# The experts' input turned by DMA for the gate's logits, and a rotary table with each value once

## The chip, the cores and the metric

The kernel runs on one core of a Trainium2 chip. The core has five engines with their own instruction queues: TensorE (PE, matmuls and transposes, with its weight loads listed as PEld), VectorE (DVE), ScalarE (ACT), GpSimd (POOL) and SyncE (SP), which here only issues DMAs. Instructions of one queue start in the order of the program; between queues semaphores order the work. The metric is the time of one execution on the device in microseconds (us); lower is better.

## The reference

One transformer block with adaptive layer norm, for 2 sequences of 2048 tokens with 256 features, all in float32:

```python
mod = (silu(c) @ wmod).reshape(2, 6, 1, -1)
sa, ca, ga, sb, cb, gb = ...                  # ga, gb: kept at least 0.25 away from 0
h = layernorm(x) * (1 + ca) + sa
x = x + ga * attention(h)                     # 2 query heads, 1 key/value head of 128, causal, rotary
h = layernorm(x) * (1 + cb) + sb
x = x + gb * experts(h)

def apply_rope(x):                            # pairs of neighbours are rotated
    out = stack([x0 * cos - x1 * sin, x1 * cos + x0 * sin])

def experts(x):                               # 8 experts, 256 -> 1024 -> 256 with gelu
    gate = softmax(x @ Wg + bg)
    thr = sigmoid(x @ Wt + bt) * 0.125
    w = (gate - thr) where it is >= 0, else 0
    out = sum over e of (w / sum(w))[e] * expert_e(x)
```

Which experts a token goes to follows from the logits `x @ Wg`, so only tokens with a weight above 0 are worked on by an expert.

## The kernel before

**First part: attention and gate.** The 4096 tokens are 32 tiles of 128 (16 for each of 2 sequences, `b` and `i`). `tile_steps(b, i, r, group, g)` adds the steps of one tile to a plan; `r` is the tile's place in the order, 0 to 31. In order: load `x` (SP), moments (`sta`, `mva` on DVE, the reciprocal root `rstda` on POOL), normalise (`xn`, line 459, DVE or POOL), two transposes on PE (`pt`, 468), copies to `hT` with scale and shift (476, 478), the projection to query, key and value (`pq`, 489), the rotation (`rot`: `t` at 505 and 513 on DVE, the addition at 522 on DVE or POOL), three transposes (`pr`, 529), scores (`psc`, 545), softmax (DVE `s`, `nmx`; ACT exponential), transposes of the weights (`ptr`, 618), their product with the values (`pav`, 628), the output projection (`po`, 662), the residual (`x`, 669) and the store of `x` to `out` (678).

Then comes what the change touches. Again moments (`stf`, `mvf`, `rstdf`), and `hx` (685, 688, DVE): the normalised, modulated row, which is the experts' input. It is used twice:

- `halves` (695, POOL) writes `hp`, in which the lower and the upper 16 bits of each float32 stand apart, 256 of the one and then 256 of the other; SP stores it to `feats` in DRAM (702). From there the second part gathers rows by token and has a DMA turn them (a DMA transposes 16-bit elements), and DVE joins the two halves to float32 again.
- `turn_h` (710, PE) transposes `hx` in two blocks of 128x128 into PSUM (`ph`), `hT2_out` (714, ACT) copies that to `hT2`, `logits` (719, PE) multiplies by the gate's weights (`pl`), and `logits_out` (727, DVE) adds the bias to `lg`.

For each group of tiles (four, later two and one) `gate_steps` turns `lg` into weights, counts the tokens of each expert and scatters entries to the experts' lists in DRAM (826, POOL).

**The order.** `Plan.run()` writes the order of all queues ahead of time. Each step has an engine (or several to choose from), a cost in us, buffers that it takes and gives back by name (`room` holds how many there are), steps that it comes after, a rank and, for a DMA, a lag (`late`) until its data is there. Simulated time goes forward, and an idle engine takes the ready step of lowest rank; a step with two engines goes to the first that is idle. These costs are numbers in the code: if one of them changes, the order on every queue may change. The run on the chip keeps the order of each queue and waits for semaphores. Work of lowest priority fills in: the first two items of expert 0 (`pha`, line 975; `pya`, 992) are computed while the last tiles of attention wait.

**Second part: the experts.** `experts()` loops over items of 256 tokens; PE alternates `h` (1202) and `y` (1193), POOL gathers and scatters rows, SP issues a DMA transpose for each item, DVE joins the halves. It begins when the list of expert 0 is complete, some 24 us after the logits of the last tile.

Of the kernel before, what the change touches and what calls it, by code (L numbers as in the profile page):

```python
# [12 lines left out]
F32 = mybir.dt.float32  # L13
BF16 = mybir.dt.bfloat16
I32 = mybir.dt.int32
U16 = mybir.dt.uint16
ET = mybir.EngineType
AF = mybir.ActivationFunctionType
ALU = mybir.AluOpType
AX = mybir.AxisListType  # L20

P = 128
B, T, D = 2, 2048, 256
HS, NH = 128, 2
E, FF = 8, 1024
KD = D // P
NF = FF // P
NT = T // P
NTOK = B * T
# [14 lines left out]
class Plan:  # L44
# [10 lines left out]
    def add(self, eng, cost, do, after=(), take=(), give=(), rank=0.0, late=0.0):  # L55

        if isinstance(eng, str):
            eng, cost, do = [eng], [cost], lambda _, do=do: do()  # L60
        self.steps.append((eng, cost, do, tuple(after), tuple(take), tuple(give), rank, late))
        return len(self.steps) - 1
# [140 lines left out]
def attention(  # L203
# [5 lines left out]
    nc = tc.nc  # L209
    PSUM = bass.MemoryType.PSUM  # L210
    ctx = ExitStack()
    room = {"ps": 6, "pav": 2, "x": 9, "s": 16, "pT": 3, "hx": 4, "hp": 3, "qT": 3, "big": 3, "xn": 3,
            "hT": 2, "hT2": 2, "aT": 2, "g_sb": 1, "sign": 1, "size": 1, "ga": 1}
    const = ctx.enter_context(tc.tile_pool(name="const_a", bufs=1))
    pool = ctx.enter_context(tc.tile_pool(name="work", bufs=3))
    small = ctx.enter_context(tc.tile_pool(name="small", bufs=8))
# [3 lines left out]
    def ps_tile(name):  # L220
        return psum.tile([P, 512], F32, tag="ps", name=name)

    def work(shape, tag, u, dtype=F32):
        return pool.tile(shape, dtype, tag=tag, name=f"{tag}{u}", bufs=room.get(tag, 3))
# [5 lines left out]
    of = {"DVE": nc.vector, "POOL": nc.gpsimd}  # L230
    first = -100.0
# [18 lines left out]
    modT = const.tile([P, 2 * KD, B], F32, name="modT")  # L250
    mod_bc = const.tile([P, B, 2 * D], F32, name="mod_bc")
    woG = const.tile([P, B, NH, D], F32, name="woG")
    rope_sb = const.tile([P, NT, 2, HS], F32, name="rope_sb")
    c_sb = const.tile([P, KD, B], F32, name="c_sb")
    sc = const.tile([P, KD, B], F32, name="sc")

# [25 lines left out]
    def load(dst, src, kb, rank=first, **how):  # L282
        return plan.add(
            "SP", max(0.5, kb / 360.0), lambda: nc.sync.dma_start(dst, src), late=2.0, rank=rank,
            **how
        )
# [5 lines left out]
    l_qkv = load(wqkv_sb, wqkvT.rearrange("(k p) f -> p k f", p=P), 512, rank=first - 1)  # L292
    l_rope = [
        load(rope_sb[:, ds(4 * q, 4)], rope.rearrange("(q n p) (z f) -> p q n z f", p=P, n=4, z=2)[:, q],
             512, rank=first if q == 0 else q * 8 - 7.5)
        for q in range(NT // 4)
    ]

# [51 lines left out]
    for b in range(B):  # L350
# [43 lines left out]
        r = 1.6 + 3 * b  # L394
# [6 lines left out]
    for e in range(RES):  # L401
# [3 lines left out]
                rank=8.0 + 4 * e,  # L405
# [12 lines left out]
    def moments(u, st, after, add):  # L418


        def stats():
            six = little([P, 6], "st", u)
            nc.vector.bn_stats(six, st["x"])
            st["mv"] = little([P, 2], "mv", u)
            nc.vector.bn_aggr(st["mv"], six)  # L425

        def rstd():
            st["rstd"] = little([P, 1], "rstd", u)
            nc.gpsimd.tensor_scalar(st["rstd"], st["mv"][:, 1:2], EPS, None, ALU.add)  # L429
            nc.gpsimd.tensor_tensor(st["rstd"], st["rstd"], neg_half, ALU.pow)  # L430

        n = add("DVE", 0.62, stats, after)
        return add("POOL", 0.85, rstd, [n])

    def tile_steps(b, i, r, group, g):

        u = f"_{b}_{i}"
        st = {}
# [4 lines left out]
        def add(eng, cost, do, after=(), **how):  # L443
            return plan.add(eng, cost, do, after=after, rank=r, **how)
# [10 lines left out]
        n_n = moments("a" + u, st, [n_x], add)  # L455
# [4 lines left out]
                st["xn"], st["x"], st["mv"][:, 0:1], st["rstd"], ALU.subtract, ALU.mult  # L460
            )

        n_n = add(["DVE", "POOL"], [0.42, 0.65], xn, [n_n], take=["xn"])

        def turn():
            st["pt"] = ps_tile(f"pt{u}")
# [13 lines left out]
        n_t = add("PE", 0.32, turn, [n_n], take=["ps"], give=["xn"])  # L480
# [18 lines left out]
        def rot(z):  # L499
            dst = st["t", z] = work([P, 3, HS], f"t{z}", u)  # L500
            table = rope_sb[:, i, z, :]
            src = st["pq"][:, : 3 * HS]
            if z == 0:
                src = src.rearrange("p (h f) -> p h f", h=3)
                nc.vector.tensor_tensor(
                    dst, src, table.unsqueeze(1).to_broadcast([P, 3, HS]), ALU.mult
                )
            else:
                src = src.rearrange("p (h j two) -> p h j two", h=3, two=2)
                d4 = dst.rearrange("p h (j two) -> p h j two", two=2)  # L510
                t4 = table.rearrange("p (j two) -> p j two", two=2)
                for y in range(2):
                    nc.vector.tensor_tensor(
                        d4[:, :, :, y], src[:, :, :, 1 - y],
                        t4[:, :, y].unsqueeze(1).to_broadcast([P, 3, HS // 2]), ALU.mult,
                    )

        n_r0 = add("DVE", 0.6, lambda: rot(0), [n_q, l_rope[i // 4]], take=["big"])
        n_r1 = add("DVE", 0.75, lambda: rot(1), [n_q, n_v, n_r0], give=["ps"])
# [16 lines left out]
        n_t = add("PE", 0.48, turn_rot, [n_r], take=["ps"], give=["big"])  # L536
# [43 lines left out]
        for h in range(NH):  # L580
            kept = []
            for c in range(nch):
# [4 lines left out]
                    give=["qT"] if (h, c) == (NH - 1, nch - 1) else [],  # L587
# [47 lines left out]
        for c0 in range(0, i + 1, 2):  # L635
# [3 lines left out]
            n_t = add(  # L639
                "PE", 0.12 * 2 * m, lambda c0=c0, m=m: turn_p(c0, m), [n_e[0, c], n_e[1, c]],  # L640
                take=["ps"] + (["pav"] if c0 == 0 else []), give=["s", "s"] if done else [],
            )
            n_o = add(
                "ACT", 0.2 + 0.26 * m, lambda c0=c0, m=m: pT_out(c0, m), [n_t], take=["pT"],
                give=["ps"],
# [35 lines left out]
        n_n = moments("f" + u, st, [n_x2], add)  # L681
# [10 lines left out]
        n_h = add("DVE", 0.97, hx, [n_n, m_mod[b], n_st], take=["hx"], give=["x"])  # L692
        def halves():
# [2 lines left out]
                st["hp"], st["hx"].bitcast(U16).rearrange("p (d two) -> p two d", two=2)  # L696
            )

        n_f = add("POOL", 1.2, halves, [n_h], take=["hp"])
        add(  # L700
            "SP", 0.8,
            lambda: nc.sync.dma_start(
                feats[ts(b * NT + i, P), :], st["hp"].rearrange("p two d -> p (two d)")
            ), [n_f], late=2.0, give=["hp"],
        )

        def turn_h():
            st["ph"] = ps_tile(f"ph{u}")
            for k in range(KD):
                nc.tensor.transpose(st["ph"][:, ts(k, P)], st["hx"][:, ts(k, P)], ident)  # L710

        def hT2_out():
            st["hT2"] = work([P, KD, P], "hT2", u)
# [12 lines left out]
                group["lg"] = little([P, 4, E + 1], "lg", u)  # L726
            nc.vector.tensor_tensor(group["lg"][:, g, :], st["pl"][:, : E + 1], bgt_sb, ALU.add)

        n_t = add("PE", 0.32, turn_h, [n_h], take=["ps"])
        n_t = add("ACT", 0.38, hT2_out, [n_t, n_f], take=["hT2"], give=["ps", "hx"])  # L730
        n_t = add("PE", 0.5, logits, [n_t, l_wg], take=["ps"], give=["hT2"])
        return add("DVE", 0.17, logits_out, [n_t, l_bg], give=["ps"])

# [119 lines left out]
    begun, q = [0] * B, 0  # L853
# [93 lines left out]
    for k in range(AHEAD):  # L947
        st = {}

        def columns(k=k, st=st):  # L950
# [4 lines left out]
            lambda c, k=k: kept.front[:, k * CI + c, 2:3].bitcast(I32), f"_{k}",  # L955
# [53 lines left out]
        for f0 in range(0, NF, 2):  # L1009
# [4 lines left out]
                take=["ps"], give=["s"] if f0 == NF - 2 else [],  # L1014
# [3 lines left out]
                take=["s"], give=["ps"],  # L1018
            ))
        n = None  # L1020
        for c in range(CI):
            for f0 in (0, NF // 2):
# [3 lines left out]
                    take=["ps"] if (c, f0) == (0, 0) else [],  # L1026
                    give=["s"] * (NF // 2) if (c, f0) == (CI - 1, NF // 2) else [],
# [424 lines left out]

def _rope_table():


    at = np.arange(0, HS, 2, dtype=np.float32)
    theta = np.float32(10000.0) ** (np.float32(-2.0) * at / np.float32(HS))
    angles = np.arange(T, dtype=np.float32)[:, None] * theta[None, :]
    cos, sin = np.cos(angles), np.sin(angles)
    both = np.stack([cos, cos], axis=-1), np.stack([-sin, sin], axis=-1)  # L1460
    return np.concatenate([a.reshape(T, HS) for a in both], axis=1).astype(np.float32)


# [35 lines left out]
```

## Time and profile before

| What | Value |
|---|---|
| Median of 5 runs | 1645.23 us (1644.44 to 1646.55) |
| The profiled execution: time, span from its first to its last instruction | 1644.22 us, 1642.4 us |
| Mean granted clock of TensorE | 0.996 |
| First part: from 0 to the first `h` matmul | 486.5 us |
| PE busy from 123 to 410 us | 284.9 of 287 us |
| `ph`: 64 transposes on PE | 12.8 us busy, 281 ns each |
| `hT2`: 32 copies on ACT | 11.8 us busy, 370 ns each |
| `hp`: 32 copies on POOL | 19.6 us busy, 612 ns each |
| Second part: `h` and `y` matmuls | 657.9 and 654.2 us busy |

How to read it: busy time of an engine is the time in which an instruction of it is listed as running. Matmuls overlap, so the listed time of one is longer than the time for which it keeps PE from the next; the distance between two starts tells more. Idle time of an engine is given with what ended it (after `<-`). "PE 9 tenths" means that at least 90% of a slice is busy.

### The profile page before, as it was taken

The numbers are of one execution on the slowest core, as the hardware profiler recorded it, in microseconds if no ns is written. First come the engines' busy times: TensorE is split into PE (matmuls) and PEld (weight loads), VectorE is DVE, ScalarE is ACT, GpSimd is POOL, SyncE is SP. The second block draws the span as 40 slices with busy tenths as digits, with TensorE's granted clock in tenths as the row PEclk, the third lists the DMA queues.
The fourth block names the chain that finished last, engine by engine and source line by source line (L and its number), as shares of the span: only waits on it lengthen the run. The fifth ranks groups of instructions, "written<-read, shape, count | busy, mean of one in ns | idle before, by whom it ended". The sixth has DMA issues, their size and how long they took to land.

```text
span 1642.4 us, 26732 instructions
## 1 busy us (share of the span) xinstructions
PE 1613.0 (98%) x7666; PEld 1346.4 (82%) x7666; DVE 656.9 (40%) x2144; ACT 584.5 (36%) x1417; POOL 908.7 (55%) x1032
## 2 busy tenths in 40 slices
PE   8999999999989999999999999999999999999997
PEld 5666776777778888888888888888888888888886
DVE  6987666666532233223223222222222232222322
ACT  3555665655532232222223222222222222222322
POOL 5575333231127767757766775675777477644443
PEclk9999999999999999999999999999999999999999
DMA  5411000010023353335335333533534343333333
GB/s 184 151 40 37 23 30 23 19 42 14 14 68 67 62 116 65 58 65 111 57 68 113 59 58 61 108 60 59 110 58 66 58 59 60 65 58 55 66 56 48
DMA packets 165950, 106.35 MB, mean 65 GB/s; under 512 B 111041, under 2 KB 157249, under 8 KB 165761
## 3 DMA queue, kind: packets, MB, share of 16 engines
q0 software_dynamic: 41968, 46.83, 17.9%
q1 hardware_dynamic: 116048, 46.22, 12.3%
q10 hardware_dynamic: 7872, 12.58, 2.4%
q8 instruction: 26, 0.43, 0.1%
q14 instruction: 36, 0.29, 0.1%
HBM read 50.39 MB, written 31.86 MB: 50 GB/s over the span
## 4 chain that ended last, share of the span: by engine, by line
PE 69%; issue 0%; DMA 0%; DVE 0%; POOLq 0%; POOL 0%; DVEq 0%
PE h L1202 35%; PE y L1193 34%; DMA out<-yo,who 0%; POOLq L1143 0%; DVE yo L1295 0%; DVE xT L924 0%; POOL out L1352 0%; DVE xT L1256 0%; DVE yb L1280 0%; DVEq L1495 0%; POOLq L1445 0%; POOLq L1352 0%; DVE who L1286 0%; POOLq L1312 0%; POOLq L1447 0%
## 5 line engine op out<-in xcount | busy, mean ns | idle before, releaser
L1202 PE MATMUL h<-xT,w 128*128 128x256 f32 (+1 forms) x2752 | 657.9, 372 | 4.8 <-DVEq L1306 4.7
L1193 PE MATMUL y<-w,g 128*128 128x256 f32 x2640 | 654.2, 379 | 0.0
L1228 ACT ACTIVATE g<-h,b_sb 128x256 f32<-128x256 f32 (+1 forms) x688 | 320.4, 466 | 835.3 <-PE h L1202 833.1
L1202 PEld LDWEIGHTS h<-xT,w 128*128 128x128 f32 x2752 | 513.0, 191 | 74.3 <-DVEq L1306 5.1
L1193 PEld LDWEIGHTS y<-w,g 128*128 128x128 f32 x2640 | 498.7, 190 | 66.2
L1352 POOL DMA_INDIRECT out<-yo,who x172 | 282.6, 1643 | 207.1 <-DVE yo L1295 154.7
L1256 DVE COPY xT<-xp 128x512 uint16<-128x512 uint16 x172 | 68.6, 440 | 609.7 <-PE h L1202 605.0
L1342 POOL DMA_INDIRECT list<-new,to x216 | 220.2, 1019 | 93.6 <-POOL new L1337 44.2
L1318 POOL DMA_INDIRECT xr<-feats,at x172 | 173.9, 1011 | 100.5 <-POOL at L1363 70.5
L545 PE MATMUL psc<-kT,qT 128*128 128x512 f32 (+3 forms) x320 | 143.4, 534 | 0.0
L628 PE MATMUL pav<-pT,v 128*128 128x256 f32 x544 | 142.6, 384 | 0.0
L628 PEld LDWEIGHTS pav<-pT,v 128*128 128x128 f32 x544 | 96.0, 190 | 29.6 <-issue 19.9
L556 DVE TENSOR_SCALAR_CACHE_REDUCE s<-psc 128x512 f32<-128x512 f32 (+3 forms) x160 | 95.2, 604 | 62.3 <-PE psc L545 48.0
L1280 DVE TENSOR_TENSOR yb<-y,b_bc 128x256 f32<-128x256 f32 x165 | 62.6, 419 | 136.1 <-PE y L1193 136.1
L572 ACT ACTIVATE s<-s,nmx 128x512 f32<-128x512 f32 (+3 forms) x160 | 103.9, 651 | 36.9 <-DVE nmx L563 36.7
L622 ACT COPY pT<-ptr 128x512 f32<-128x512 f32 (+1 forms) x144 | 76.5, 564 | 51.7 <-PE pav L628 33.2
L826 POOL DMA_INDIRECT list<-entry,place x40 | 42.5, 1063 | 72.7 <-DVE place L823 43.4
L1271 DVE SCALAR_TENSOR_TENSOR gate<-gb_bc,mcur,part 128x256 f32<-128x256 f32 x172 | 75.8, 481 | 3.0
L618 PEld LDWEIGHTS ptr<-ident,s 128*128 128x128 f32 x544 | 63.4, 142 | 14.3 <-ACT s L572 4.6
L618 PE MATMUL ptr<-ident,s 128*128 128x128 f32 x544 | 72.4, 274 | 2.1 <-ACT s L572 1.9
L1363 POOL COPY at<-sheet 128x2 int32 x85 | 63.7, 749 | 14.7 <-DMA xp<-xr 14.7
L429 POOL TENSOR_SCALAR rstdf<-mvf 128x1 f32<-128x1 f32 x32 | 8.5, 264 | 113.6 <-DVE mvf L425 86.4
(165 smaller groups left out, 1101.4 us busy)
## 6 DMA issues: line engine op xcount, KB each, us to landing
w<-in_w ACTq DMA_DIRECT2D x12, 1024.0 KB, 7.9
x<-in_x SPq DMA_DIRECT2D x32, 128.0 KB, 2.1
out<-x SPq DMA_DIRECT2D x32, 128.0 KB, 1.7
feats<-hp SPq DMA_DIRECT2D x32, 128.0 KB, 1.7
w<-in_w SPq DMA_DIRECT2D x4, 1024.0 KB, 8.5
list<-new,to POOLq DMA_INDIRECT x216
xr<-feats,at POOLq DMA_INDIRECT x172
out<-yo,who POOLq DMA_INDIRECT x172, 3.9
```

The costliest lines, as they stand in the source:

```text
L545: nc.tensor.matmul(ps[:, :w], st["qT"][:, h, :], kT[:, ds(c * SC, w)], start=True, stop=not last)
L556: nc.vector.tensor_scalar(s[:, :w], st["sc", h, c][:, :w], 1.0, None, ALU.mult, ALU.max, accum_out=st["mx", h][:, c : c + 1],)
L572: nc.scalar.activation(s[:, :w], s[:, :w], AF.Exp, bias=st["nmx", h], accum_out=st["den"][:, h, c : c + 1],)
L618: nc.tensor.transpose(ptr[:, j, h, :], s[:, ds((c0 + j) * P % SC, P)], ident)
L622: nc.scalar.copy(pT[:, :m], st["ptr", c0][:, :m])
L628: nc.tensor.matmul(st["pav"][:, : NH * P], v[:, c0 + j, :], st["pT", c0][:, j].rearrange("p h t -> p (h t)"), start=(c0 + j == 0), stop=(c ...
L1193: last = pe.matmul(ys[c], gs[f % 4][:, ts(c, P)], weights[e][1][:, f, :], start=(f == 0), stop=(f == NF - 1),)
L1202: last = pe.matmul(hs[f % 4][:, :w], weights[e][0][:, k, ts(f, P)], xT[:, k, :w], start=(k == 0), stop=(k == KD - 1),)
L1228: act.activation(gs[f % 4][:, :w], hs[f % 4][:, :w], AF.Gelu_apprx_tanh, bias=b1_sb[:, at : at + 1],).then_inc(sem["act"], 1)
L1318: pool.indirect_dma_start(out=xr[:, ts(c, 2 * D)], out_offset=None, in_=feats, in_offset=bass.IndirectOffsetOnAxis(ap=at[:, c : c + 1], ax ...
L1342: pool.indirect_dma_start(out=lists[e], out_offset=bass.IndirectOffsetOnAxis(ap=to[:, j : j + 1], axis=0), in_=new[:, j, :], in_offset=Non ...
L1352: pool.indirect_dma_start(out=rows, out_offset=bass.IndirectOffsetOnAxis(ap=who[:, c : c + 1], axis=0), in_=yo[:, c, :], in_offset=None, b ...
```

## The change

For the first 28 tiles (`r < 28`) the experts' input is no longer transposed by PE. A DMA on SP's queue transposes `hp`, which is there in 16-bit halves anyway, into `hpT` (four blocks of 128x128), and POOL, or DVE if POOL is not idle in the plan, joins the halves to float32 in `hT2`. The last four tiles keep the old way. In the plan the transpose comes after the store of `hp` to `feats`; `hx` is given back after `halves` and `hp` after the transpose.

The rotary table keeps each cosine and sine once (64 + 64 values a token instead of 128 + 128). The rotation's first product reads the cosines with a repeat of two; its second product makes the sign itself, with a scalar_tensor_tensor for even places and a tensor_tensor for odd places, where there were two tensor_tensors before.

Two costs in the plan change: `xn` on POOL from 0.65 to 1.3 us, and `halves` from 1.2 to 0.8 us (and its store from 0.8 to 0.5).

```diff
-            "hT": 2, "hT2": 2, "aT": 2, "g_sb": 1, "sign": 1, "size": 1, "ga": 1}
+            "hT": 2, "hT2": 2, "hpT": 2, "aT": 2, "g_sb": 1, "sign": 1, "size": 1, "ga": 1}
...
-    rope_sb = const.tile([P, NT, 2, HS], F32, name="rope_sb")
+    rope_sb = const.tile([P, NT, 2, HS // 2], F32, name="rope_sb")
...
-             512, rank=first if q == 0 else q * 8 - 7.5)
+             256, rank=first if q == 0 else q * 8 - 7.5)
...
-        n_n = add(["DVE", "POOL"], [0.42, 0.65], xn, [n_n], take=["xn"])
+        n_n = add(["DVE", "POOL"], [0.42, 1.3], xn, [n_n], take=["xn"])
...
         def rot(z):
             dst = st["t", z] = work([P, 3, HS], f"t{z}", u)
             table = rope_sb[:, i, z, :]
-            src = st["pq"][:, : 3 * HS]
+            src = st["pq"][:, : 3 * HS].rearrange("p (h j two) -> p h j two", h=3, two=2)
+            d4 = dst.rearrange("p h (j two) -> p h j two", two=2)
             if z == 0:
-                src = src.rearrange("p (h f) -> p h f", h=3)
                 nc.vector.tensor_tensor(
-                    dst, src, table.unsqueeze(1).to_broadcast([P, 3, HS]), ALU.mult
+                    d4, src,
+                    table.unsqueeze(1).unsqueeze(3).to_broadcast([P, 3, HS // 2, 2]), ALU.mult,
                 )
             else:
-                src = src.rearrange("p (h j two) -> p h j two", h=3, two=2)
-                d4 = dst.rearrange("p h (j two) -> p h j two", two=2)
-                t4 = table.rearrange("p (j two) -> p j two", two=2)
-                for y in range(2):
-                    nc.vector.tensor_tensor(
-                        d4[:, :, :, y], src[:, :, :, 1 - y],
-                        t4[:, :, y].unsqueeze(1).to_broadcast([P, 3, HS // 2]), ALU.mult,
-                    )
+                t3 = table.unsqueeze(1).to_broadcast([P, 3, HS // 2])
+                nc.vector.scalar_tensor_tensor(
+                    d4[:, :, :, 0], src[:, :, :, 1], -1.0, t3, ALU.mult, ALU.mult
+                )
+                nc.vector.tensor_tensor(d4[:, :, :, 1], src[:, :, :, 0], t3, ALU.mult)
...
-        n_f = add("POOL", 1.2, halves, [n_h], take=["hp"])
-        add(
-            "SP", 0.8,
+        by_dma = r < NTOK // P - 4
+        n_f = add("POOL", 0.8, halves, [n_h], take=["hp"], give=["hx"] if by_dma else [])
+        n_hp = add(
+            "SP", 0.5,
             lambda: nc.sync.dma_start(
                 feats[ts(b * NT + i, P), :], st["hp"].rearrange("p two d -> p (two d)")
-            ), [n_f], late=2.0, give=["hp"],
+            ), [n_f], late=2.0, give=[] if by_dma else ["hp"],
         )
...
+        def turn_halves():
+            st["hpT"] = work([P, 2 * KD, P], "hpT", u, U16)
+            nc.sync.dma_start_transpose(st["hpT"], st["hp"].rearrange("p two d -> p (two d)"))
+
+        def join_halves(eng):
+            st["hT2"] = work([P, KD, P], "hT2", u)
+            of[eng].tensor_copy(
+                st["hT2"].bitcast(U16).rearrange("p k (t two) -> p k t two", two=2),
+                st["hpT"].rearrange("p (two k) t -> p k t two", two=2),
+            )
...
-        n_t = add("PE", 0.32, turn_h, [n_h], take=["ps"])
-        n_t = add("ACT", 0.38, hT2_out, [n_t, n_f], take=["hT2"], give=["ps", "hx"])
+        if by_dma:
+            n_t = add("SP", 1.3, turn_halves, [n_f, n_hp], late=2.2, take=["hpT"], give=["hp"])
+            n_t = add(
+                ["POOL", "DVE"], [0.65, 0.45], join_halves, [n_t], take=["hT2"], give=["hpT"]
+            )
+        else:
+            n_t = add("PE", 0.32, turn_h, [n_h], take=["ps"])
+            n_t = add("ACT", 0.38, hT2_out, [n_t, n_f], take=["hT2"], give=["ps", "hx"])
         n_t = add("PE", 0.5, logits, [n_t, l_wg], take=["ps"], give=["hT2"])
...
-    cos, sin = np.cos(angles), np.sin(angles)
-    both = np.stack([cos, cos], axis=-1), np.stack([-sin, sin], axis=-1)
-    return np.concatenate([a.reshape(T, HS) for a in both], axis=1).astype(np.float32)
+    return np.concatenate([np.cos(angles), np.sin(angles)], axis=1).astype(np.float32)
```

## The prediction

> **What bounds the kernel now.** I read the page first: busy shares and the slices of the span.
>
> ```profile
> span 1642.4 us, 26732 instructions
> PE 1613.0 (98%) x7666; PEld 1346.4 (82%) x7666; DVE 656.9 (40%) x2144; ACT 584.5 (36%) x1417; POOL 908.7 (55%) x1032
> ...
> PE   8999999999989999999999999999999999999997
> PEld 5666776777778888888888888888888888888886
> DVE  6987666666532233223223222222222232222322
> ```
>
> TensorE (PE) is busy nearly everywhere. There are two regimes: to about 486 us (the first twelve digits) attention, with VectorE (DVE) at 6 to 9 tenths, then the experts, with VectorE at 2 to 3. All edits lie in the first. The experts' work depends on the tokens, not on when it starts, so I carry it over unchanged. So the question is when the last attention tile reaches its logits.
>
> The table of windows splits the first regime (columns: window, length, busy time of PE, PEld, DVE, ACT, POOL, granted clock, DMA share, GB/s).
>
> ```profile
> 41.00:82.00 41.00, 40.21 (x201) 27.81 (x200) 37.30 (x140) 23.09 (x72) 20.83 (x35) 1.00 0.45 152
> 82.00:123.00 41.00, 40.51 (x204) 28.17 (x202) 35.52 (x130) 23.07 (x67) 29.74 (x43) 1.00 0.13 40
> 123.00:164.00 41.00, 40.05 (x197) 28.62 (x197) 29.67 (x109) 21.63 (x64) 20.93 (x30) 1.00 0.12 37
> 369.00:410.00 41.00, 40.44 (x203) 29.33 (x202) 25.15 (x103) 24.40 (x66) 7.96 (x11) 1.00 0.04 14
> ```
>
> From 123 us on only PE is full. From 41 to 123 us PE leaves 0.8 + 0.5 us, and DVE only 3.7 + 5.5 us: two engines are nearly full there. That decides how much of a saving on PE arrives.
>
> The timeline shows the last tile: what the change would replace, and what a step costs.
>
> ```profile
> 454.82 5.34 PE L975 MATMUL pha<-s_x,w 128*128 128x256 f32 x24
> 455.02 1.00 DVE L669 SCALAR_TENSOR_TENSOR x<-po,rd,x 128x256 f32<-128x256 f32 x2 [4.50 <-PE po L662]
> 457.99 0.48 DVE L688 SCALAR_TENSOR_TENSOR hx<-hx,rstdf,mod_bc 128x256 f32<-128x256 f32 x1 [0.77 <-POOL rstdf L430]
> 458.54 0.61 POOL L695 COPY hp<-hx 128x512 uint16<-128x512 uint16 x1 [0.58 <-DVE hx L688]
> 459.18 0.33 SPq L702 DMA_DIRECT2D feats<-hp  x1
> 460.00 0.38 PE L710 MATMUL ph<-ident,hx 128*128 128x128 f32 x2
> 460.21 1.89 PE L975 MATMUL pha<-s_x,w 128*128 128x256 f32 x8
> 460.93 0.37 ACT L714 COPY hT<-ph 128x256 f32<-128x256 f32 x1
> 461.94 0.51 PE L719 MATMUL pl<-wgt_sb,hT 128*128 128x9 f32 x4
> 462.31 1.97 PE L992 MATMUL pya<-w,s_g 128*128 128x256 f32 x8
> ```
>
> Two readings. The two transposes of `hx` are listed with 0.38 us, but the next matmul starts 0.21 us after them: matmuls overlap, so PE is given back 0.21 us a tile. And from the end of the projection (455.0) to the logits (461.94) a tile takes 6.9 us; PE does other work meanwhile.
>
> **The change part by part.**
>
> *PE's transposes go, for 28 of 32 tiles.* 28 x 0.21 = 5.9 us of PE. The groups by form add what PE idled before them:
>
> ```profile
> L710 PE MATMUL ph<-ident,hx 128*128 128x128 f32 x64 | 12.8, 281 | 2.0 <-DVE hx L688 1.4 <-DVE rd L605 0.4
> L714 ACT COPY hT<-ph 128x256 f32<-128x256 f32 x32 | 11.8, 370 | 4.4 <-PE ph L710 4.3
> ```
>
> Of the 2.0 us about 1.7 belong to the 28 tiles. Together -7.6 us. ScalarE loses 28 copies of 0.37 us, 10.4 us off the path (ACT is busy 55 to 60% there), worth nothing. The PSUM buffers of `ph` come free for other steps; no wait of PE for a PSUM buffer is over 0.5 us in the list of waits, so nothing again.
>
> *The new way to the logits.* Per tile: the transpose on SP's queue, then a join. Their nearest rows are the two transposes of the expert's first items, which are twice as large:
>
> ```profile
> 340.39 1.35 SPq L918 DMA_TRANSPOSE sign_p<-g_sb_r  x1
> 344.24 0.74 DVE L924 COPY s_x<-sign_p 128x512 uint16<-128x512 uint16 x2
> ```
>
> 3.85 us from issue to the join; a plain 128 KB store of `feats` lands in 1.7 us, so the new one is between 1.7 and 3.85, and I take 3.85, of the same kind. A join is one 128x512 uint16 copy: 0.42 us on DVE (L924), 0.61 on POOL if it is like `halves` (L695). For the last tile's timing: `feats` is issued until 459.5, the transpose is joined at 463.4, on POOL until 464.0, that is 9.0 us after the projection instead of 6.9. In the built order of the changed kernel, PE has 11.2 to 18.8 us of other work between a projection and its logits for these 28 tiles (counted with the slots above: 0.11 us a transpose, 0.22 us a 256-column matmul); before, it had 5.6 to 10.9. The margin is at least 2.2 us, mostly 3 to 5. So I cost the longer way at nothing; it is hidden by that work, and without the cover a tile pays up to 2.1 us (9.0 - 6.9). The transposed tiles' `hp` buffers (three) are held some 4 us longer against some 14 us between tiles: nothing.
>
> *SP's queue.* 28 more issues of 1.35 us, 38 us over 400, on a queue that mostly waits. Behind each stand the store of `x` and the next load of `x`, 1.4 us later; a load is 2 us and is used tiles later. Nothing. In front stand stores that wait for DVE; the built order puts each transpose after its own `feats` and before or just after one such store, so a late tile can hold it. That is the rival below.
>
> *POOL* gets 19 joins (11.6 us) and loses three `xn` (3.7) and two additions (2.0): +5.9 us at a share of 51 to 73% early, 20 to 50% later. While it waits for a transposed tile, the reciprocal roots (`rstd`) and scatters behind it wait too; the planner's own costs and lags put the join 6.4 us after `halves`, and the rows above give 4.2 (459.15 to 463.4), so I take nothing.
>
> *DVE* gets 9 joins, six of them in the first eleven tiles, that is before 123 us. The rotation's first half becomes a scalar_tensor_tensor: I price it by two rows, 0.48 us for 128x256 (L669) against 0.42 for a tensor_tensor (L1280), so +0.06 us a tile; the broadcast cosine keeps its 384 elements and I give it 0. With the planner's new choices up to there (one `xn` more, two additions more at 0.56, one `hT` less) DVE has 6 x 0.42 + 11 x 0.06 + 0.41 + 1.12 - 0.41 = 4.3 us more before 123 us. It had 9.2 us free from 41 on; its share goes from 89 to about 95%. Bounds: 0 (all of it falls in idle time) to 4.3 (DVE is the bound there). Two nearly full engines do not fill each other's gaps, so I take the middle, +2.2.
>
> *The rotary table* is halved, 1 MB less to load. At the start DMA runs at 290 GB/s, and before the third loads 0.25 MB less lie in the queue, 0.9 us. PE's first wait is for `wm`, which is loaded ahead of it. Between -0.8 and 0; I take 0.
>
> Sum: -5.9 - 1.7 + 2.2 = -5.4 us. The profiled execution took 1644.2 us (span 1642.4, 1.8 around it); it becomes 1638.8. The median of the five runs, 1645.2, lies 1.0 above it, so 1639.8.
>
> [...] On the row: a 128x128 transpose costs PE 0.11 us, and the DMA's way 3.85 us for eight blocks of 16 bits. [...]
>
> **The rivals.** A difference under 0.2% (3.3 us: 1641.9 to 1648.5) can't be told from no change.
>
> *DVE becomes the bound to 123 us.* For it: 95% busy, and a DVE copy beside POOL can be held:
>
> ```profile
> 108.55 1.58 DVE L459 TENSOR_SCALAR xn<-x,mva,rstda 128x256 f32<-128x256 f32 x1 [0.46 <-PE pt L468]
> 108.96 1.01 POOL L522 TENSOR_TENSOR t<-t,t 128x384 f32<-128x384 f32 x1
> ```
>
> That `xn` takes 0.41 us when alone; it ended with POOL's addition. Against it: PE, too, has less to do. Price: all 4.3 us, and up to 1.17 for some of the six joins: +4 to +8, a result of 1642 to 1646.
>
> *The join comes late (slower).* At one place: PE stands at `pl` until the join, because the transpose waits on SP behind a store of another tile's `x`. It decides once the queues add more than the margin, 2.2 to 5 us; beyond it every microsecond is paid 28 times. At 0.5 us a tile, +14 - 7.6 = +6.4: 1651.6. For it: SP's queue keeps its order, and its stores wait up to 19.6 us for DVE. Against it: they wait in program order, and that order was laid out with the transposes in it.
>
> *Only the later tiles gain.* Nothing arrives before 123 us, 19 tiles are left: 19 x 0.21 = -4.0, 1641.2.
>
> **How the numbers follow.** The forecast 0.55, only the later tiles 0.13, DVE the bound 0.17, a late join 0.15. The forecast's own range is 1636.8 (DVE's work free and the start 0.8 us earlier) to 1641.9 (all 4.3 us of it paid). Below, the range takes in the 1.3 us that PE leaves idle from 41 to 123 us, should the new order fill them too; above, it leaves out most of the late join: 1635.5 to 1647.5. Faster: 0.55 + 0.12 = 0.67; same: 0.18 (mostly the DVE case); slower: 0.15.
>
> **What would show it.** Right: `ph` x8, the first `h` matmul near 481 us instead of 486.5, `pl` with almost no idle before it, and PE busy 99% from 123 to 410 us. DVE's windows to 123 us near 39 of 41 with PE below 40 would mean DVE binds. Wrong: idle time of PE before `pl`, released by `hT<-hpT`; or joins on POOL with the idle before them ended by the transpose and `rstd` late behind them; or transposes that take more than 4 us to land.

## The result and the profile after

The changed kernel takes 1647.15 us (median of 24 runs, 1640.26 to 1650.06); the kernel before took 1645.13 us beside it (44 runs, 1643.42 to 1647.28). The ratio is 1.0009 (95% interval 1.0003 to 1.0014): slower by a hair, where 1639.8 us was forecast. The profiled execution took 1641.42 us, near the low end of a spread of 10 us, so it shows what the change gains and not what it usually loses. For that, another execution of the same program is shown below (e9_after).

The page of the changed kernel (busy time of each engine, then tenths in 40 slices):

```profile
span 1638.7 us, 26663 instructions
PE 1607.7 (98%) x7610; PEld 1341.3 (82%) x7610; DVE 661.2 (40%) x2162; ACT 574.8 (35%) x1385; POOL 916.0 (56%) x1046
...
PE   8999999999989999999999999999999999999997
PEld 5667776767778888888888888888888888888886
DVE  6887756666532333223223222232222232222322
```

PE has 56 matmuls and 5.3 us less than before. VectorE has 4.3 us more over the whole span, but not early: to 123 us it is busy for 99.2 us, and 101.3 before. The windows of the first part (window, length, busy time of PE, PEld, DVE, ACT, POOL, granted clock, DMA share, GB/s):

```profile
41.00:82.00 41.00, 39.06 (x195) 26.84 (x194) 35.73 (x140) 22.52 (x71) 25.51 (x42) 1.00 0.57 173
82.00:123.00 41.00, 40.17 (x190) 27.47 (x189) 35.43 (x134) 22.61 (x68) 30.50 (x43) 1.00 0.23 61
123.00:164.00 41.00, 41.00 (x209) 30.07 (x208) 30.59 (x121) 24.36 (x70) 24.04 (x34) 1.00 0.15 40
369.00:410.00 41.00, 40.96 (x206) 30.11 (x205) 24.35 (x103) 24.30 (x64) 6.59 (x10) 1.00 0.06 18
```

From 41 to 123 us PE now idles 1.94 + 0.83 = 2.8 us (1.3 before), with VectorE no busier (71.2 us; 72.8 before). The last two windows look better (0.00 and 0.04 us of idle time, 0.95 and 0.56 before), but they are not typical: over the whole stretch from 123 to 410 us PE is busy for 284.7 of 287 us, and for 284.9 before. The share of 99% that the prediction named as a sign was there before the change too, so it tells nothing. The new operations, by their tile (duration in ns: least, median, greatest), with who waited for them:

```profile
L714 SPq DMA_TRANSPOSE hpT<-hp x28: 1200/1200/2782, 41.4 to 384.4; - x28
L718 POOL COPY hT<-hpT x19: 655/662/894, 65.7 to 387.0; 128x512 uint16<-128x512 uint16 x19
L718 DVE COPY hT<-hpT x9: 395/418/1282, 46.2 to 276.5; 128x512 uint16<-128x512 uint16 x9
...
  PEld pl L730: 4.1, 4
  PE pl L730: 1.7, 3
...
DMA to landing us min/median/max: 2.4/2.4/4.1
```

PE itself waited for a join in three places, 1.7 us in all. One transpose took 4.1 us to land, just over the 4 us that the prediction named as a sign of being wrong. The list of PE's waits to 470 us (total, times, longest):

```profile
PE ph L710 <- DVE hx L686: 2.3, 1, 2.3
PE pl L730 <- POOL hT L718: 1.2, 2, 1.1
PE ptr L616 <- ACT s L570: 1.1, 1, 1.1
PE pl L730 <- DVE hT L718: 0.5, 1, 0.5
```

The longest wait at `pl` has this story in the timeline:

```profile
344.36 1.24 SPq L935 DMA_TRANSPOSE sign_p<-g_sb_r  x1
...
346.36 2.78 SPq L714 DMA_TRANSPOSE hpT<-hp  x1
...
350.89 1.09 POOL L926 DMA_INDIRECT g_sb_r<-feats,front  x1 [4.93 <-DMA feats<-hp]
...
353.25 0.67 POOL L718 COPY hT<-hpT 128x512 uint16<-128x512 uint16 x1
...
353.97 0.61 PE L730 MATMUL pl<-wgt_sb,hT 128*128 128x9 f32 x4 [1.07 <-POOL hT L718]
```

The transpose follows that of the expert's first items and its issue takes 2.78 us instead of 1.2. The join then stands on GpSimd behind gathers, the first of which waits 4.93 us for the store of `feats`. It is the rival "the join comes late", in one place instead of 28.

So the first part does gain. The logits of the last tile start at 459.1 us (461.9 before), the first `h` at 483.4 us (486.5 before). Up to those logits PE is busy for 444.5 us (449.1 before) and idle for 14.5 (12.8 before). What is missing in the median is lost after the first `h`. The execution e9_after of the same program took 1645.35 us; its first `h`:

```profile
481.22 3.38 PE L1219 MATMUL h<-xT,w 128*128 128x256 f32 x9 [4.47 <-DVEq L1323]
```

That is 5.3 us earlier than before (the sum of the prediction was -5.4). Its chain of waits at the change from expert 3 to expert 4 (start, length, what):

```profile
1027.30 2.59 PE y L1210 x12
1029.89 3.86 issue
1033.75 4.24 PE h L1219 x12
1037.98 1.17 PE y L1210 x4
1039.15 0.86 PE h L1219 x4
```

PE stands still for 3.86 us and waits for nothing that the profile shows ("issue"). The twelve `h` matmuls after it take 4.24 us instead of 2.59. In its windows:

```profile
1020.00:1030.00 10.00, 9.89 (x46) 8.36 (x44) 0.90 (x3) 2.37 (x5) 7.11 (x10) 1.00 0.37 58
1030.00:1034.00 4.00, 0.25 (x1) 0.26 (x2) 3.08 (x9) 0.00 (x0) 2.90 (x3) 1.00 1.13 288
1034.00:1041.00 7.00, 7.00 (x26) 5.85 (x26) 0.03 (x1) 1.90 (x4) 2.63 (x4) 0.76 1.01 207
1041.00:1048.00 7.00, 7.00 (x34) 6.17 (x33) 0.77 (x2) 1.90 (x4) 4.96 (x8) 1.00 0.15 38
```

After the stand the granted clock is 0.76 over 7 us, and 26 matmuls start instead of 34. In the kernel before, `h` follows `y` there without a pause (it starts at 1035.44 us, and the last `y`, listed from 1032.85 us for 2.75, end at 1035.60). From the first `h` to the end of the span it is 1155.9 us before, 1155.3 in the execution of the changed kernel without the stand, and 1161.5 in e9_after. The account of e9_after against the profiled execution before: -5.3 to the first `h`, +5.6 from there, +0.8 outside the span (2.65 us instead of 1.8); together +1.1, and 1645.35 - 1644.22 is 1.13.

### The profile page after: what moved, and what is told of

It is laid out like the page before. It is cut to its first block, busy times and chain, and to the rows that moved or that the text cites. A ratio compares the mean times of both kernels' runs of the same rounds, so it can differ in the third digit from the quotient of the medians.

```text
span 1638.7 us, 26663 instructions
## 1 busy us (share of the span) xinstructions
PE 1607.7 (98%) x7610; PEld 1341.3 (82%) x7610; DVE 661.2 (40%) x2162; ACT 574.8 (35%) x1385; POOL 916.0 (56%) x1046
## 4 chain that ended last, share of the span: by engine, by line
PE 69%; issue 0%; DMA 0%; POOLq 0%; DVE 0%; POOL 0%; DVEq 0%
PE h L1219 35%; PE y L1210 35%; DMA out<-yo,who 0%; POOLq L1160 0%; DVE yo L1312 0%; DVE xT L941 0%; POOL out L1369 0%; DVE yb L1297 0%; DVEq L1509 0%; POOLq L1462 0%; POOLq L1369 0%; DVE who L1303 0%; POOLq L1464 0%; POOLq L1329 0%; POOLq L1330 0%
## 5 line engine op out<-in xcount | busy, mean ns | idle before, releaser
L543 PEld LDWEIGHTS psc<-kT,qT 128*128 128x128 f32 x320 | 57.7, 190 | 15.3 <-issue 7.3
```

What stands on the lines that cost most here:

```text
L543: nc.tensor.matmul(ps[:, :w], st["qT"][:, h, :], kT[:, ds(c * SC, w)], start=True, stop=not last)
```

## The experiments

Batches of one chip each; "before" is the kernel before on the same chip. Places in the code are counted in PE's instruction stream of the built program, in instructions modulo 256. That about 256 of them come with one transfer of the instruction queue q8 (16384 bytes in the traces) is an estimate that takes q8 for PE's: 18 such transfers start up to the first `h`, and PE has some 2200 matmuls by then, each with its weight load, so 244 to a transfer. In all versions the eight expert loops start 258 instructions apart, so a kernel is described by the places of its first and last loop: 130 to 144 before, 19 to 33 after.

**First batch (before: 1645.01 us, 29 runs): the parts alone.**

e1_again is the changed kernel unaltered.

> The changed kernel unaltered, for the trace of another of its executions. The one profiled so far took 1641.4 us at a mean clock of 0.997, 5.7 us less than the median of 1647.2; most executions have 0.993 to 0.995. Theory 'clock': the work of TensorE is 6 us shorter in each, but in most executions one or two more stretches at half clock follow idle time of TensorE late in the attention part; then this trace, if it is of a typical execution (span near 1645), shows the first h matmul still before 484 us or so, one or two more rows at half clock (each about 3.4 us, as the rows of the traces so far are 3.4 and 6.8 us), and the same instructions with the same waits otherwise. Theory 'late joins': typical executions wait longer for the joins, so the trace shows over 3 us of idle time of TensorE before pl, released by the join of the halves. Ratio to before 1.000 to 1.002.

1647.25 us (1640.83 to 1649.64), ratio 1.0007 (0.9997 to 1.0018). Its profiled execution took 1649.64 us and showed the stand first: 3.84 us at 1033.10, and then a granted clock of 0.51 from 1035 to 1042 us.

e2_rope puts only the halved table and its rotation into the kernel before; e3_cost only the planner's cost of `xn`.

```diff
 e2_rope: before, with
-    rope_sb = const.tile([P, NT, 2, HS], F32, name="rope_sb")
+    rope_sb = const.tile([P, NT, 2, HS // 2], F32, name="rope_sb")
 ... and rot() of the change
 e3_cost: before, with
-        n_n = add(["DVE", "POOL"], [0.42, 0.65], xn, [n_n], take=["xn"])
+        n_n = add(["DVE", "POOL"], [0.42, 1.3], xn, [n_n], take=["xn"])
```

> The kernel before with the halved rotary table alone, and the new form of the rotation. Theory 'clock' and theory 'late joins' both expect little: between -1 us (0.25 MB less ahead of the early loads) and +1 us (0.06 us more of VectorE for each of 32 tiles). More than 2 us either way would mean that the order of the work, which changes with the table's cost in the plan, matters in itself.

> The kernel before with one number changed: the plan's cost of the normalised input on GpSimd, 0.65 to 1.3 us. No instruction is added or removed; only the order changes and where xn runs. Theory 'clock' and 'late joins': within 2 us of before. If the third theory holds, that any new order costs idle time of TensorE here or there and so decides more than the 6 us of transposes, this one differs by more than 2 us from before.

e2_rope: 1645.1 us, ratio 1.0000 (0.9991 to 1.0008). e3_cost: 1644.32 us, 0.9998 (0.9990 to 1.0007). Neither part does anything alone. The second product of the rotation in the changed kernel, by its tile, against the form that it replaces:

```profile
L511 DVE SCALAR_TENSOR_TENSOR t<-pq,rope_sb x32: 325/349/359, 16.1 to 369.5; 128x192 f32<-128x192 f32 x32
L514 DVE TENSOR_TENSOR t<-pq,rope_sb x32: 341/347/349, 16.3 to 369.8; 128x192 f32<-128x192 f32 x32
```

349 ns, as the tensor_tensor of before (median 349): the 0.06 us a tile that the prediction gave it are not there.

e4_dma_old_cost is the changed kernel with the old cost of `xn`, which gives 24 joins to GpSimd and 4 to VectorE.

```diff
-        n_n = add(["DVE", "POOL"], [0.42, 1.3], xn, [n_n], take=["xn"])
+        n_n = add(["DVE", "POOL"], [0.42, 0.65], xn, [n_n], take=["xn"])
```

> The change without its new cost of xn on GpSimd (0.65 us in the plan as before), with the transposes by DMA and the halved table. In this order VectorE makes 4 of the 28 joins instead of 9, and GpSimd 24. Theory 'late joins' expects it slower than the change (GpSimd is the busier engine early, and a join waits in its queue): +2 to +6 us. Theory 'clock' expects a time that follows the idle time of TensorE late in the part, so anything from -4 to +4, with a clock of 0.996 where there is no gap over 2 us before 478 us.

1654.13 us, 1.0063 (1.0050 to 1.0077). Here the first part is what loses: the first `h` comes at 493.1 us, and PE waits

```profile
PE pr L527 <- POOL t L520: 2.9, 1, 2.9
PE ptr L616 <- DVE lg L738: 2.6, 1, 2.6
PE pt L468 <- POOL xn L459: 2.3, 1, 2.3
```

5.2 us for GpSimd's addition and `xn`, and 2.6 us for VectorE's addition of the bias to the logits. The cost of `xn` does nothing without the transposes on DMA (e3_cost) and 6.9 us with them (1654.13 against 1647.25). GpSimd has 25 `xn` and 24 joins in this order, 23 and 19 in the changed kernel; that its longer queue is the cause is likely from the waits, but not shown alone, since the whole order differs. (The loops lie at 9 to 23 here, so part of the 1654 may be the place, though the profiled execution, 1652.55 us, has no stand between experts 3 and 4.)

**Second batch: the place of the code.** Theory: the gain is lost because the shorter program moves the experts' code. Rival: the change gains too little, in the first eleven tiles above all. Matmuls of one column at the start move the code and do nothing else; the order of all other instructions stays. These four ran on another chip, on which the kernel before takes 1663.1 us (29 runs), so they are compared with each other and with that.

```diff
+    def pad():
+        idle = ps_tile("idle")
+        for _ in range(55):                    # e6: 72, e7: 34
+            nc.tensor.matmul(idle[:, :1], ones, ones[:, :1], start=True, stop=True)
+    plan.add("PE", 0.01, pad, take=["ps"], give=["ps"], rank=first - 50)
```

e5_after_pad is the changed kernel with the loops where the kernel before has them; e6_before_shift is the kernel before with the loops where the changed one has them.

> The change with 55 one-column matmuls (110 instructions) on TensorE at the start, while it waits for its first weights; every other instruction and its order are as in the change. They put the experts' loops back where they stood in the program of before relative to blocks of 256 instructions (16 KB, the size of the transfers in the instruction queue): the loops begin 130 to 144 instructions into a block, in the change 19 to 33. Theory 'code': the time lost in typical executions of the change is TensorE waiting for its instructions where one expert's loop ends and the next begins (3.8 us in the trace of e1_again, and 3.4 us more by half clock behind it). Then this kernel has no idle time of TensorE there and a median of 1641 to 1643.5, a ratio of 0.998 to 0.999. Theory 'attention': the loss is in the attention part; then padding changes nothing, median 1647 and a ratio of 1.001.

> The kernel before with 72 one-column matmuls (144 instructions) at the start, which put the experts' loops where the change has them (19 to 33 instructions into a block of 256). Nothing else changes. Theory 'code': this one gets the change's loss without the change: a median of 1648 to 1651, spread over some 8 us instead of 4, a clock of 0.993 to 0.995 and idle time of TensorE between two experts in its trace, if that is of a typical execution. Theory 'attention': 1645 to 1646, as before.

e5_after_pad: 1656.53 us, 0.9966 (0.9951 to 0.9982), with no stand between experts 3 and 4. e6_before_shift: 1672.13 us, 1.0068 (1.0049 to 1.0086), and the stand appears in the old kernel. Its timeline at that place, PE only:

```profile
1045.63 2.32 PE L1199 MATMUL y<-w,g 128*128 128x256 f32 x10
1053.18 3.35 PE L1208 MATMUL h<-xT,w 128*128 128x256 f32 x7 [5.24 <-issue]
```

The same place in the program, 5.24 us; nothing of the change is in that kernel. Both kernels move in the direction that the place asks for.

e7_late_pad and e8_late leave the first eleven tiles on PE (`by_dma = 11 <= r < NTOK // P - 4`), with loops at 139 to 153 (34 pads) and at 70 to 84 (none).

> The change for the tiles from the 12th to the 28th alone (17 tiles), with 34 one-column matmuls at the start so that the experts' loops begin 139 to 153 instructions into a block, as before. It tells what the first eleven tiles are worth: VectorE and TensorE are both nearly full up to 123 us, and the trace of the change has 3.3 us more of lost TensorE time there than before. If those tiles give nothing, this kernel is as fast as e5 or up to 1.5 us faster (17 x 0.21 = 3.6 us of transposes less, median 1641 to 1642.5). If they do give their 2.3 us, it is 2 us slower than e5 (1643.5 to 1645).

> e7 without the matmuls at the start: the experts' loops begin 70 to 84 instructions into a block, so that each loop (140 instructions) lies within one block, as in the change, where before it reached into the next. Theory 'code': where the loop lies within one block the next expert's code is not there in time in most executions; 3 to 6 us slower than e7, with idle time of TensorE between two experts. If what counts is another place of the code than the loop's end, this one equals e7.

e7_late_pad: 1664.84 us, 1.0013 (0.9997 to 1.0029); e8_late: 1665.20 us, 1.0018 (1.0006 to 1.0030). The 17 later tiles alone bring nothing, which speaks against "only the later tiles gain". What the first eleven tiles are worth stays open: the last tile's logits start at 462.0 us in e7 and at 457.6 in e5, but at 466.4 in e8, which has e7's order, so single traces on this chip differ by as much; and e7's order has waits of its own:

```profile
PE ph L716 <- DVE hx L692: 3.1, 3, 1.9
...
PE pl L736 <- POOL hT L724: 1.5, 1, 1.5
```

e8 shows no stand and equals e7, so 70 to 84 is a harmless place too.

**Third batch (before: 1645.07 us, 17 runs): the size on one chip.** e9_after is the changed kernel, e10_pad_130 is e5 again, e11_pad_70 has 25 pads.

> The changed kernel, unaltered, as the yardstick of this batch. Theory (place of the experts' code): where the 3.8 us stand of PE between y of expert 3 and h of expert 4 comes, followed by 6.8 us at half clock, an execution takes about 1648, where it does not, about 1641; the median lies between. Rival (chance, or the chip): the same spread of times in all kernels of the batch, padded or not.

> The changed kernel with 55 matmuls of one column at the start, which put the experts' loops where the kernel before has them (130 to 144 modulo 256 instructions). [...] Theory: the stand never comes, so the time is that of an execution of the changed kernel without the stand, about 1641.4, plus at most 3.7: 1641 to 1645, with a narrow spread; below the yardstick of the batch by 2 to 6 us. Rival (the place of the code does not matter): yardstick plus 0 to 3.7 us, about 1649 to 1651.

> The changed kernel with 25 such matmuls, the loops at 70 to 84 modulo 256. [...] If only the places 19 to 33 are bad, it is 2.0 us below the kernel with 55 pads (30 x 0.067). If a loop that lies across the end of a 256-instruction block is bad wherever it starts, it is at the yardstick plus 1.7, about 1649. If the place does not matter, it lies between the other two by its number of pads.

e9_after: 1645.05 us (1641.09 to 1650.08), 0.9999 (0.9989 to 1.0009). e10_pad_130: 1639.13 us (1638.14 to 1639.68), 0.9961 (0.9949 to 0.9974). e11_pad_70: 1638.17 us, 0.9956 (0.9943 to 0.9968). The pads bring 5.9 and 6.9 us, and the spread shrinks from 9 us to 1.5 and 3.3. From the first `h` on e10 takes 1155.2 us, e9 1161.5. e10's chain where e9 stands:

```profile
1028.62 2.59 PE y L1216 x12
1031.21 2.59 PE h L1225 x12
1033.80 0.86 PE y L1216 x4
```

I had given 55 pads 3.7 us, 0.067 each, and no run shows either number; the row has 1.62 us, 0.03 each, and they cost nothing. e10's timeline of PE at the start:

```profile
3.08 1.62 PE L322 MATMUL idle<-ones 128*128 128x1 bf16 x55 [3.08 <-POOL ones L267]
6.53 2.69 PE L339 MATMUL pm<-sc,wm 128*128 128x2 f32 x12 [1.82 <-DMA wm<-in_wmod]
```

They run in the 6.8 us in which PE waits for its first load anyway (`pm` starts at 6.84 us in the first profile of the changed kernel, at 6.53 here). Nor do they speed up the first part: the first `h` is at 482.2 us in e10 and at 481.2 in e9, which has none.

e12_join_dve_pad takes the later joins off GpSimd.

```diff
-                ["POOL", "DVE"], [0.65, 0.45], join_halves, [n_t], take=["hT2"], give=["hpT"]
+                ["POOL", "DVE"] if r < 11 else ["DVE"], [0.65, 0.45] if r < 11 else [0.45],
+                join_halves, [n_t], take=["hT2"], give=["hpT"]
 ... and 58 pads
```

> The changed kernel with the joins of the later tiles on VectorE alone (23 on VectorE, 5 on GpSimd, before 9 and 19) and 58 pads, so that the loops start at 129 to 143. It takes the join of the waits before the logits out from behind GpSimd's gather. If that queue behind the gather is what costs the waits before the logits (2.2 to 2.4 us), it is 1 to 2 us below the kernel with 55 pads. If VectorE, which gets 14 joins of 0.42 us more (5.9 us), pays for them elsewhere, it is level with that kernel or up to 4 us above it.

1638.32 us (1637.84 to 1640.31), 0.9961 (0.9948 to 0.9974): level with e10 and e11. PE's waits at `pl` for the joins are 1.4 us in three places, 0.9 in two in e10 (1.7 in three in the first profile of the changed kernel). Taking the late joins off GpSimd brings nothing that can be measured.

**Fourth batch (before: 1645.31 us, 14 runs): which places are bad.** The changed kernel with 8, 40, 75 and 103 pads.

> The changed kernel with 8 pads: the loops of the experts start at 36 to 50 modulo 256 instructions. After the last pass of expert 3's loop, PE jumps from about 182 to 38 of the next block of 256. If every jump from the first part of a block into the next is bad, it stays like the unpadded kernel: 1641 to 1650, median 1645, with the stand of 3.8 us. If the bad places are a narrow band round 19 to 33, it takes 1637 to 1640.

> The changed kernel with 40 pads: loops at 100 to 114. Expert 3's loop ends at about 246 and the jump goes to 102 of the next block. Both theories say that it takes 1637 to 1640 as with 25 and 55 pads; a stand here would say that the crossing alone is what costs.

> The changed kernel with 75 pads: loops at 170 to 184. Each loop lies across the end of a block (176 to 60 of the next), and the jump after it stays within the next block. If a loop that is split between two blocks costs something in each pass, it is slower by many small stands; else 1637 to 1640.

> The changed kernel with 103 pads: loops at 226 to 240, split 30 to 110 between two blocks; the jump after expert 3's loop goes from 116 to 228 of one block. The pads last about 3.1 us and still end before the load that PE waits for first. If no jump crosses a block, no stand: 1637 to 1640.

e9_after, e11_pad_70 and e10_pad_130 are of the third batch, the others of the fourth.

| Loops start at (mod 256) | Kernel | Median us (lowest to highest) | Ratio to before (95%) |
|---|---|---|---|
| 19 to 33 | e9_after | 1645.05 (1641.09 to 1650.08) | 0.9999 (0.9989 to 1.0009) |
| 36 to 50 | e13_pad_36 | 1641.15 (1638.06 to 1645.95) | 0.9979 (0.9963 to 0.9996) |
| 70 to 84 | e11_pad_70 | 1638.17 (1636.62 to 1639.96) | 0.9956 (0.9943 to 0.9968) |
| 100 to 114 | e14_pad_100 | 1640.07 (1638.40 to 1641.37) | 0.9969 (0.9956 to 0.9981) |
| 130 to 144 | e10_pad_130 | 1639.13 (1638.14 to 1639.68) | 0.9961 (0.9949 to 0.9974) |
| 170 to 184 | e15_pad_170 | 1638.96 (1638.24 to 1640.27) | 0.9963 (0.9949 to 0.9978) |
| 226 to 240 | e16_pad_226 | 1639.67 (1638.24 to 1642.13) | 0.9965 (0.9952 to 0.9977) |

Each of the five places from 70 on gives a median of 1638 to 1640 us. 36 lies between: two of its six runs took 1644 and 1646, the profiled one has no stand. Loops that are split between two blocks of 256 (170, 226) took 1638.96 and 1639.67 us, and a jump into the next block from loops at 70 or 100 left 1638.17 and 1640.07 us, against 1639.13 at 130. So of the seven places the bad ones are the two lowest, and neither "the loop must lie in one block" nor "every jump into the next block is bad" describes it.

**What the stand is.** The switch from expert 3 to 4 is the only one at which the body for a single tile of 128 tokens, some 110 instructions, is jumped over; the traces show that body at the end of the other experts and not of this one. From loops at 19 to 33 that jump goes from about place 168 to about 21 of the next block of 256. The traffic of e9_after between 1030 and 1034 us, by queue (packets, MB, share of 16 engines):

```profile
q10 hardware_dynamic: 316, 1.06, 88.9%
q1 hardware_dynamic: 296, 0.08, 21.7%
q8 instruction: 1, 0.02, 1.5%
q0 software_dynamic: 32, 0.00, 0.6%
```

In the stand one instruction transfer of 16 KB arrives, among a load of weights on q10 (1.06 MB, 88.9% of the engines' time); the same view of e1_again and of e6_before_shift shows one in the stand, too.

It is a transfer that comes far earlier where there is no stand. Queue q8 makes 26 transfers of 16384 bytes in each profile (27 in e6_before_shift, with its 72 pads; the pages of the changed kernel and of e9_after list the 25 within the span), 18 (19) of them up to the first `h`. That q8 carries PE's code is my reading, as no view names the engine: the 72 pads, which are on PE alone, add one transfer, and a q8 transfer comes in each stand of PE. From the first `h` to the switch it lists in the changed kernel's first profile (484 to 1029 us):

```profile
q8 instruction: 3, 0.05, 0.0%
```

and in e9_after (482 to 1029 us):

```profile
q8 instruction: 2, 0.03, 0.0%
```

In all 15 profiles without a stand the third transfer starts at 870 to 918 us, over 120 us before the switch (892.6 us in the changed kernel's first profile). In the three with a stand it is late and starts inside it: at 1031.1 us in e9_after, 1034.3 in e1_again and 1050.4 in e6_before_shift. It takes 0.9 us there, and PE goes on 1.7 to 1.8 us after its end. (e10_pad_130 has a transfer at 1033.0 us without a stand, but that is its fourth; its third came at 871.3.) So PE stands while that transfer comes (in e9_after from 1029.89 to 1033.75 us). That it stands because its next code is not there yet is my reading; the traces name nothing that ends the stand ("issue"). No run shows a rule that parts 19 and 36 from 70 and 100. Shown is that moving the code, with the order left alone, puts the stand in and takes it out, and that the stand goes with the late third transfer; why that transfer is late in some executions and places is not shown.

## Why the prediction was wrong

**The step that failed** is in the first paragraph: "The experts' work depends on the tokens, not on when it starts, so I carry it over unchanged." The work is unchanged, its time is not: 1161.5 us in e9_after instead of 1155.9, since 111 instructions fewer ahead of it put its code in a place where, in some executions, PE stands at the switch from expert 3 to 4 (3.86 us in e9_after, 3.84 in e1_again). With the code put right, the kernel takes 1638.2 to 1640.1 us (places from 70 on, on two chips where the kernel before takes 1645.1 and 1645.3), round the 1639.8 forecast. That it fits to 1 us is partly luck: the first part gained less than forecast (below). "1.8 around it" failed with it: 2.65 to 2.74 us in e9_after, e1_again and the first profile.

**PE's transposes, -5.9: about right.** PE's busy time up to the last logits fell by 4.6 us in the first profile and by 5.4 in e9_after (443.7 us), for 56 matmuls less with 0.11 us between two starts (6.1 us).

**The idle time before them, -1.7: went there and came back elsewhere.** The waits of 0.9, 0.4 and 0.4 us at `ph` of before are gone. In their place PE waits at `pl` (1.7 us, 0.8 in e9_after) and for the softmax (1.1 us at one `ptr`), and at one `ph` of the last four tiles for 2.3 us. With VectorE's term the forecast was 0.5 us more of idle time (-1.7 + 2.2); up to the last logits it grew by 1.7 us in the first profile and by 0.4 in e9_after.

**VectorE to 123 us, +2.2: near in size by luck, the reason wrong.** PE's idle time from 41 to 123 us grew by 1.5 us (1.2 in e9_after), but VectorE is not at 39 of 41 us; it is at 35.7 and 35.4, and instead of 4.3 us more it has 2.1 us less to 123 us. The largest waits of PE there are for ScalarE's softmax (1.1 us at `ptr`, 0.5 at `pav`, 0.3 at `psc`) and for one join on VectorE (0.5). "DVE becomes the bound" falls. "Only the later tiles gain" has e7 against it; besides, with eleven tiles before 123 us, 17 are left and not 19, so its price was -3.6 us and not -4.0.

**The longer way hidden at nothing: nearly right.** 25 of 28 joins keep PE from nothing, and the transposes land in 2.4 us where I took 3.85 to the join. Three places cost 1.7 us, and in e12, with the late joins on VectorE, nothing is gained that can be measured. The slower rival named late joins, 28 times 0.5 us; the slower result came from elsewhere.

**The rotary table, 0: right** (e2, 1.0000). **The row set against the change** (0.11 us of PE for a transpose, 3.85 us for the DMA's way) decided nothing: with 56 transposes moved to the DMA and the code in a good place the kernel takes 1638.2 to 1640.1 us, and the DMA's 2.4 us to landing stayed off the path but for the three waits (1.7 us in the first profile).

**The sum to the first `h`.** -5.4 forecast; over the nine profiles of this order on the chips of the first, third and fourth batches and of the first result, the first `h` is at 481.2 to 484.0 us, median 482.2: -4.3. The nine differ by 2.8 us among themselves, and the kernel before has one trace here, so the missing 1.1 us are not traced to a single wait.

**Open:** the rule by which a place is bad; why the third transfer on q8 is late in some executions of one program (e1_again, e9_after) and not in others (the first profile, 1641.42 us); and what the extra 0.9 us outside the span are. They follow the place of the code as well, as the last section shows.

## What to carry to other kernels

A part of the program that the edit did not touch changed its time here: with its run-time loops and jumps shifted by 111 instructions, the experts took 1161.5 us in e9_after instead of 1155.9. When an edit of a few us comes out as nothing, compare the trace piece by piece up to a common point, look for a pause labelled "issue" in the untouched part, and take a second profile if the runs spread. Then repeat the measurement with some idle instructions ahead of the loops, in a place where the engine waits anyway: here 25 to 103 one-column matmuls turned a ratio of 0.9999 to 1.0009 into 0.996 to 0.997. The profile's count of instruction transfers in the untouched part went with it: up to the switch two in e9_after, which has the stand, and three in the first profile, which has none.

## What the runs showed of the hardware

- A stand of PE at a run-time jump: 3.84, 3.86 and 5.24 us, with one 16 KB instruction transfer in it that came over 120 us before the jump in the 15 profiles without a stand, and then a granted clock of 0.76 (e9_after, 1034 to 1041 us) or 0.51 (e1_again, 1035 to 1042 us).
- The granted clock did not follow from a pause alone. After the 2.33 us wait at `ph` (it ends between 436 and 439 us) it was 0.66 from 437 to 442 us in e1_again and 1.00 in e9_after and the first profile, in the same program.
- Time outside the span went with the place of the code. It is 1.8 to 2.2 us in all kernels with loops from 70 on, 2.0 to 3.1 us in the executions of the changed kernel, and 3.5 us in three of the six runs of e13_pad_36 (2.1 in the others). The old kernel has 1.8 to 1.9 us in e2_rope and e3_cost, with its code in place, and 2.0 to 2.9 us in e6_before_shift, where only the pads, and with them the place, differ. What it consists of, no run shows.
- 55 one-column bf16 matmuls are listed with 1.62 us, 0.03 us each; the expectations had 0.067, which no row here shows.
- A DMA transpose of 128x512 16-bit elements took 1.2 us to issue and landed in 2.4 us (medians of 28 in the first profile of the changed kernel), and its issue took 2.78 us in the one case that came two microseconds behind another one.
